# Graph attention with a mixture of experts on one core: flags between partitions prepared ahead, one scan for both directions, and the experts' layer norm on ScalarE

## The chip, the cores and the metric

The kernel runs on one core of one Trainium2 chip. The metric is the device time of one launch in microseconds; the time before is the median of three runs. Readings of the trace come from one more execution, which the hardware profiler recorded.

## What the reference computes

There are 30000 nodes with 256 features, 510000 edges sorted by their destination, 8 edge types and 4 heads. The layer is a graph attention followed by a small mixture of experts, each with a layer norm in front and a residual around it:

```python
feat = einsum('ni,rhid->rnhd', layernorm(x), conv_weights)      # one feature table per edge type
el = sum(feat[type, src] * attn_l[type]);  er = sum(feat[type, dst] * attn_r[type])
e  = leaky_relu(el + er, 0.2)
alpha = softmax of e over the edges that share a destination     # segment_max, exp, segment_sum
x  = x + segment_sum(alpha * feat[type, src]) + h_bias
y  = layernorm(x)
x  = x + shared_mlp(y) + (best 2 of 4 experts by softmax(y @ gW + gb), weighted)(y)
```

All results are f32.

## The kernel before, in words

**Features.** For every 128 nodes the kernel normalises x, transposes it (L292) and multiplies it with the weights of all types and heads (L305); the tables go to memory as `feat`, with one more column per head that holds the node's share of the score. Beside this, generators are advanced by hand through `aside`: `edge_records` prepares the records of the edges, `places` then works out in 21 batches of up to 12 blocks what each block of edges needs later, and `expert_weights` loads the experts. `places` writes one row of `WR` words per partition and block into `rk_d`: the row numbers to gather (`WI`), destinations (`WD`), marks (`WA`), penalties (`WP`), flags (`W1`) and types (`WT`). `first_rows` gathers the first edge row of each partition and block ahead of time and stores it in `stage`, four blocks to a store.

**Blocks.** Then 252 blocks of 2048 edges follow, 16 edges (`U`) on each of 128 partitions, and one last block (`UL` = 18). Edges of one destination lie next to each other, so they may run over several of a partition's columns and over several partitions. The softmax needs the largest score of a destination: `scores` runs one scan forward and one backward along the columns (L1033, L1034), with penalties of -1e30 where a destination starts. The value at the end of each partition's row is then passed on between partitions: `turn_ends` transposes 128x4 values for each direction (L1040, L1041), `across` scans 4x128 values forward (L1047) and backward (L1048), `turn_back` transposes both back (L1055, L1056), and `softmax` combines them (L1062 to L1065). For the scan over partitions, `flags_across` transposes a flag for each partition, which says that one destination fills it (L962), and copies it to `through` (L964); `flags` lays out the penalties and flags for it by four copies on ScalarE (L951, L952, L954, L955).

After the exponential (`exps`, L1071, with the copy L1072 into `ft`) the gathered rows are weighed on VectorE (L1079), one-hot matrices are made on ScalarE (L1010, L1011), and TensorE sums the rows by destination (L1086). `finish` divides, `residual_sum` adds x (L1117) and takes the statistics for the second layer norm (`stats`, L722 and L723).

**Order.** The program's order is written out by hand. Each block t has six slots. In slot 0 come `load(t + 2)`, `gather(t + 1)` and `flags(t + 1)`, in the later slots the steps of block t, and with each slot goes a sixth of the sums of block t - 1. `load` puts five DMAs into SP's queue (`rk` L903, `dr` L921, `erp` L924, `xt` L926 and `stage` L931 by `gather`), and `gather` 15 indirect DMAs into POOL's (L933), into a ring of four blocks' rows.

**Experts.** Four blocks share one pass of the experts. `Experts.steps` lists its steps, and one of them is taken in each slot once a group's last x1 is there: the square root (`spread`, L727), the scaling in two steps (`scale`, L731 and L734), two transposes (`turn`, L742, copied by ScalarE at L744), the layers (`layer`: matmuls L798, eviction with relu on ScalarE L799), the gates (L764 to L786), `experts2` (L823, L825, L829), the weighing (L838), and four times `last` (L851 to L854), whose result L857 adds to x1 and `put` (L1097) sends to the output from SP's queue.

The code after the blocks runs only if a flag found in the data asks for it; it did not in these runs.

Of the kernel before, what the change touches and what calls it, by code (L numbers as in the profile page):

```python
# [21 lines left out]
P = 128  # L22
# [22 lines left out]

WI, WD, WA, WP, W1, WT, WR = 0, U, 2 * U, 3 * U, 4 * U + 1, 6 * U + 3, 6 * U + 3 + U * 4

# [6 lines left out]
def kernel(  # L54
# [46 lines left out]
    dk_d = dram.tile([NBLK * CAP + 16], I16, name="dk_d")  # L101
    stage = dram.tile([NBLK * P, H * HW], F32, name="stage")
    exc_d = dram.tile([P], F32, name="exc_d")
    KT = -(-(NBLK + 1) // P)
# [25 lines left out]
    def layernorm(pool, xg, n, name, m=P):  # L130
# [10 lines left out]
        for t in range(n):  # L141
# [31 lines left out]
                   allow_small_or_imprecise_dtypes=True)  # L173
    NPEN = 3
    pens = []
    for i in range(NPEN + 1):
        f = wf.tile([P, H, U if i < NPEN else UL], F32, name=f"penf{i}")
        b = wf.tile([P, H, U if i < NPEN else UL], F32, name=f"penb{i}")
        nc.gpsimd.memset(f, -BIG)
        nc.gpsimd.memset(b, -BIG)  # L180
        pens.append((f, b))
    carry = []
    for i in range(2):
        cf = wf.tile([H, P + 1], F32, name=f"carf{i}")
        cb = wf.tile([H, P + 1], F32, name=f"carb{i}")
        nc.gpsimd.memset(cf, -BIG)
        nc.gpsimd.memset(cb, -BIG)
        carry.append((cf, cb))
    nc.gpsimd.memset(b3, 0.0)
# [32 lines left out]
    with ExitStack() as cx:  # L222
# [268 lines left out]
        def places(cl):  # L491
# [30 lines left out]
            fetch(0)  # L522
            yield
            done = None
            for k, (b0, n) in enumerate(batches):
# [32 lines left out]
                count["ready"] = b0 + n  # L558
                pen = kp.tile([P, GB, UW], F32, name="penk")[:, :n]
                nc.vector.tensor_scalar_mul(pen, rc[:, :, :, 3], -BIG)  # L560
                yield
                nc.gpsimd.tensor_copy(of[:, :, WP:WP + UW], pen)
                d16 = kp.tile([P, GB, U], I16, name="d16k")[:, :n]
                nc.gpsimd.tensor_copy(d16, rc[:, :, :U, 1])
                a1 = kp.tile([P, GB, UW], F32, name="a1k")[:, :n]
                a2 = kp.tile([P, GB, UW], F32, name="a2k")[:, :n]
                flat = "p b u -> p (b u)"
# [5 lines left out]
                nc.gpsimd.tensor_copy(of[:, :, W1:W1 + UW], a1)  # L573
                nc.gpsimd.tensor_copy(of[:, :, W1 + UW:W1 + 2 * UW], a2)
                yield
                th = o[:, :, WT:].bitcast(BF16).rearrange("p b (u r) -> p b u r", r=R)
# [5 lines left out]

                def done(o=o, d16=d16, b0=b0, n=n):
                    nc.sync.dma_start(rk_d[b0:b0 + n].rearrange("b p w -> p b w"), o)
                    nc.sync.dma_start(dk_d[b0 * CAP:(b0 + n) * CAP].rearrange("(b p u) -> p b u", p=P, u=U), d16)
# [18 lines left out]
        def first_rows():  # L604

            n, kept = 4, []
            fp = cl.enter_context(tc.tile_pool(name="first", bufs=3))
# [94 lines left out]
    class Experts:  # L702
# [3 lines left out]
        def __init__(self, pool, ph, pc, x1, n, put):  # L706
            self.pool, self.ph, self.pc, self.x1, self.n, self.put = pool, ph, pc, x1, n, put
            self.w = n * M
            self.mv = pool.tile([P, T, 2], F32, name="c_mv", bufs=2)

# [9 lines left out]
        def stats(self, t):  # L720
            st = self.pool.tile([P, 6], F32, name="c_st")
            nc.vector.bn_stats(st[:M], self.x1[:M, t, :])  # L722
            nc.vector.bn_aggr(self.mv[:M, t, :], st[:M])  # L723

        def spread(self):
            self.rs = self.pool.tile([P, T], F32, name="c_rs")
            nc.scalar.activation(self.rs[:M, :self.n], self.mv[:M, :self.n, 1], AF.Sqrt, bias=eps[:M])  # L727

        def scale(self, j):
            if j == 0:  # L730
                nc.vector.reciprocal(self.rs[:M, :self.n], self.rs[:M, :self.n])  # L731
                self.xn = self.pool.tile([P, T, D], F32, name="c_xn")
            for t in range(j, min(j + 2, self.n)):
                nc.vector.tensor_scalar(self.xn[:M, t, :], self.x1[:M, t, :], self.mv[:M, t, 0:1],  # L734
                                        self.rs[:M, t:t + 1], op0=ALU.subtract, op1=ALU.mult)

# [125 lines left out]
    with ExitStack() as cx:  # L862
# [16 lines left out]
        NCH = 6  # L879
        flat = "p h u -> p (h u)"  # L880
        blk = {}

        class Block:


            def __init__(self, t):
                self.u = U if t < NBLK else UL
                self.sc = [-(-self.u * c // NCH) for c in range(NCH + 1)]
                self.dw = -(-self.u * P // 48) * 16
                self.dc = [-(-self.u * c // 4) for c in range(5)]  # L890
                at = t % RING * U
                self.ft = ring[:, at:at + self.u]
                self.own = t < NBLK
                self.pens = pens[t % NPEN if t < NBLK else NPEN]

        def load(t):
# [3 lines left out]
            if s.own:  # L900
# [6 lines left out]
                s.mark, s.marki = rf[:, WA:WA + U], rk[:, WA:WA + U]  # L907
                s.pen = rf[:, WP:WP + U + 1]

# [27 lines left out]
        def flags(t):  # L937


            s = blk[t]  # L940
            n = s.u
            s.penf, s.penb = s.pens
            if not s.own:
                s.pen = wk.tile([P, UL + 1], F32, name="pen", bufs=1)[:, :n + 1]
                nc.vector.tensor_scalar_mul(s.pen, s.rc[:, :, 3], -BIG)
                s.a12 = wk.tile([P, 2, UL], F32, name="a12", bufs=1)
                nc.vector.tensor_tensor_scan(s.a12[:, 0], s.pen[:, :n], s.pen[:, :n], 0.0, ALU.min, ALU.min)
                nc.vector.tensor_tensor_scan(s.a12[:, 1, ::-1], s.pen[:, n:0:-1], s.pen[:, n:0:-1], 0.0,
                                             ALU.min, ALU.min)
            mid = s.pen[:, None, 1:n].to_broadcast([P, H, n - 1])  # L950
            nc.scalar.copy(s.penf[:, :, 1:], mid)  # L951
            nc.scalar.copy(s.penb[:, :, :n - 1], mid)  # L952
            ends = wk.tile([P, 2, H], F32, name="ends")
            nc.scalar.copy(ends[:, 0, :], s.a12[:, 0, n - 1:n].to_broadcast([P, H]))  # L954
            nc.scalar.copy(ends[:, 1, :], s.a12[:, 1, 0:1].to_broadcast([P, H]))  # L955
            s.ends = ends

        def flags_across(t):
            s = blk[t]
            pn = ps_p.tile([H, 2, P], F32, name="pn", tag="sm")  # L960
            for i in range(2):
                nc.tensor.transpose(pn[:, i, :], s.ends[:, i, :], ident)  # L962
            s.through = wk.tile([H, 2, P], F32, name="through")
            nc.scalar.copy(s.through, pn)  # L964
# [59 lines left out]
        def scores(t):  # L1024
# [4 lines left out]
            exchange(s, s.e)  # L1029
            s.fb = wk.tile([P, 2, H * UL], F32, name="fb")[:, :, :H * s.u].rearrange("p i (h u) -> p i h u", h=H)  # L1030
            s.f, s.b = s.fb[:, 0], s.fb[:, 1]
            e, f, b = s.e.rearrange(flat), s.f.rearrange(flat), s.b.rearrange(flat)
            nc.vector.tensor_tensor_scan(f, s.penf.rearrange(flat), e, -BIG, ALU.add, ALU.max)  # L1033
            nc.vector.tensor_tensor_scan(b[:, ::-1], s.penb.rearrange(flat)[:, ::-1], e[:, ::-1], -BIG,  # L1034
                                         ALU.add, ALU.max)

        def turn_ends(t):
            s = blk[t]
            s.t1 = ps_p.tile([H, 2, P], F32, name="t1", tag="sm")
            nc.tensor.transpose(s.t1[:, 0, :], s.f[:, :, s.u - 1], ident)  # L1040
            nc.tensor.transpose(s.t1[:, 1, :], s.b[:, :, 0], ident)  # L1041

        def across(t):

            s = blk[t]
            cf, cb = carry[t % 2]
            nc.vector.tensor_tensor_scan(cf[:, 1:], s.through[:, 0, :], s.t1[:, 0, :], -BIG, ALU.add, ALU.max)  # L1047
            nc.vector.tensor_tensor_scan(cb[:, P - 1::-1], s.through[:, 1, ::-1], s.t1[:, 1, ::-1], -BIG,  # L1048
                                         ALU.add, ALU.max)

        def turn_back(t):
            s = blk[t]
            cf, cb = carry[t % 2]
            s.t2 = ps_p.tile([P, 2, H], F32, name="t2", tag="sm")
            nc.tensor.transpose(s.t2[:, 0, :], cf[:, :P], ident[:H, :H])  # L1055
            nc.tensor.transpose(s.t2[:, 1, :], cb[:, 1:], ident[:H, :H])  # L1056

        def softmax(t):
# [3 lines left out]
            nc.vector.tensor_add(c, s.t2[:, :, :, None].to_broadcast(at), s.a12[:, :, None, :s.u].to_broadcast(at))  # L1062
            nc.vector.tensor_max(c, c, s.fb)
            nc.vector.tensor_max(s.f, c[:, 0], c[:, 1])
            nc.vector.tensor_sub(s.e, s.e, s.f)  # L1065
            exchange(s, s.e)
# [338 lines left out]
```

## Time and profile before

| | us |
|---|---|
| median of three runs (8380.45 to 8390.53) | 8389.48 |
| the profiled execution | 8380.65 |
| its span, first to last instruction | 8379.0 |
| busy: PE / DVE / ACT / POOL | 6330.2 / 5381.4 / 3416.7 / 4073.5 |
| mean granted TensorE clock | 0.877 |

PE is TensorE's matmuls, PEld its weight loads (which overlap), DVE VectorE, ACT ScalarE, POOL GpSimd and SP the queue that issues most DMAs. The span is the profiled execution without what lies around it. An idle time in the profile stands with the event that ended it ("releaser"); "remote" and "issue" are waits for which the profile shows no instruction of the program. The features reach to about 1750 us, and the blocks fill the rest; in the page's slices of 1/40 of the span this is slices 1 to 8 and 9 to 40.

### The profile page before, as it was taken

How to read it: one execution, taken by the hardware profiler on the slowest of the kernel's cores; microseconds unless marked ns; L12 is line 12 of the kernel's file. 1: busy time of each engine (PE TensorE's matmuls, PEld its weight loads, DVE VectorE, ACT ScalarE, POOL GpSimd, SP SyncE). 2: the span in 40 equal slices, each digit the busy share in tenths (PEclk: the TensorE clock that was granted, in tenths of full speed). 3: DMA queues.
4: the chain of work that ended last, by engine and by line, in shares of the span. 5: the costliest groups of instructions: out<-in, count | busy, mean ns of one | idle time of the engine just before them, and what ended most of it. 6: DMA issues, size and time to landing. Idle time of an engine off the chain costs nothing. (4 is left out here: it accounts for less than half of the span.)

```text
span 8379.0 us, 96556 instructions
## 1 busy us (share of the span) xinstructions
PE 6330.2 (76%) x25254; PEld 3986.0 (48%) x25255; DVE 5381.4 (64%) x13882; ACT 3416.7 (41%) x9511; POOL 4073.5 (49%) x4327
## 2 busy tenths in 40 slices
PE   9999999956666767777666667777666777777667
PEld 5555555534444444444444444444444444444444
DVE  5557774447666666666666666666666666666665
ACT  2222222224444444444444444444444444444444
POOL 1101114665555555555555555555555555555552
PEclk9999999978888888888888888888888888888888
DMA  6657778964444444444444444444444444444441
GB/s 226 229 177 238 224 243 303 341 197 123 116 117 117 118 116 119 119 121 119 117 120 117 119 116 118 118 123 118 118 116 117 118 119 118 116 119 117 115 118 55
DMA packets 761457, 1209.52 MB, mean 144 GB/s; under 512 B 241638, under 2 KB 599789, under 8 KB 730685
## 3 DMA queue, kind: packets, MB, share of 16 engines
q1 hardware_dynamic: 565453, 663.56, 24.8%
q0 software_dynamic: 194400, 539.40, 23.3%
q8 instruction: 206, 3.38, 0.2%
q14 instruction: 358, 2.93, 0.1%
q10 hardware_dynamic: 1040, 0.26, 0.0%
HBM read 818.57 MB, written 384.23 MB: 144 GB/s over the span
## 5 line engine op out<-in xcount | busy, mean ns | idle before, releaser
L933 POOL DMA_INDIRECT ft<-feat,rk x3798 | 3608.6, 950 | 2919.9 <-PE po L1086 956.0
L1086 PE MATMUL po<-ft,oh 128*128 128x260 f32 x8100 | 2305.4, 421 | 286.3 <-DVE ho L1107 149.5
L1086 PEld LDWEIGHTS po<-ft,oh 128*128 128x128 f32 x8100 | 1565.4, 208 | 569.7 <-issue 292.4
L305 PE MATMUL ps<-w,xT 128*128 128x448 f32 (+1 forms) x4700 | 1712.6, 519 | 14.3 <-DVE xT L294 8.6
L1079 DVE TENSOR_TENSOR ft<-ft,p 128x768 f32<-128x768 f32 x1518 | 1289.9, 850 | 394.8 <-issue 184.1
L1010 ACT ACTIVATE oh<-icol,rk 128x128 f32<-128x128 f32 x4032 | 1329.1, 389 | 66.4 <-remote 45.5
L305 PEld LDWEIGHTS ps<-w,xT 128*128 128x128 f32 x4700 | 877.3, 191 | 704.9 <-issue 613.5
L798 PE MATMUL ph<-xT,w 128*128 128x512 f32 (+1 forms) x512 | 372.1, 859 | 961.8 <-issue 888.7
L307 ACT COPY fo<-ps 128x448 f32<-128x448 f32 (+1 forms) x711 | 377.3, 533 | 1087.4 <-PE ps L305 912.4
L998 DVE TENSOR_TENSOR ere<-pe,rk 128x384 f32<-128x384 f32 x1008 | 553.3, 549 | 373.4 <-remote 247.9
L1011 ACT ACTIVATE oh<-oh 128x384 f32<-128x384 f32 x1518 | 740.2, 488 | 49.4
L987 PEld LDWEIGHTS <-ohT 128*128 128x128 bf16 x4050 | 393.9, 158 | 548.8 <-issue 438.1
L798 PEld LDWEIGHTS ph<-xT,w 128*128 128x128 f32 x512 | 112.3, 260 | 1112.1 <-issue 952.5
L744 ACT COPY xT<-ph 128x512 f32<-128x512 f32 (+1 forms) x128 | 73.1, 572 | 1325.3 <-remote 1299.9
L1000 DVE TENSOR_REDUCE e<-ere 128x16 f32<-128x384 f32 (+1 forms) x1012 | 561.5, 555 | 34.8
L987 PE MATMUL pe<-erp,ohT 128*128 128x96 bf16 x4050 | 442.3, 236 | 113.3 <-DVE ohT L970 73.5
L798 PE MATMUL ph<-xT,v 128*128 128x512 f32 (+1 forms) x1024 | 500.2, 613 | 2.3 <-ACT h L799 1.5
L1062 DVE TENSOR_TENSOR c<-t,rk 128x128 f32<-128x128 f32 x252 | 71.8, 285 | 618.9 <-remote 582.0
L1071 ACT ACTIVATE p<-e 128x64 f32<-128x64 f32 (+1 forms) x253 | 70.4, 278 | 844.9 <-DVE e L1022 741.8
L307 DVE COPY fo<-ps 128x448 f32<-128x448 f32 (+1 forms) x464 | 242.3, 528 | 221.9 <-PE ps L305 194.2
L1040 PE MATMUL t<-ident,fb 128*4 128x128 f32 x253 | 70.8, 280 | 383.6 <-DVE fb L1033 196.7
L851 PE MATMUL pf<-w,h 128*128 128x256 f32 x506 | 203.2, 491 | 189.1 <-ACT wT L844 85.1
(206 smaller groups left out, 7422.2 us busy)
## 6 DMA issues: line engine op xcount, KB each, us to landing
feat<-fo SPq DMA_DIRECT2D x234, 1040.0 KB
dr<-dk_d SPq DMA_DIRECT2D x252, 516.0 KB
ft<-feat,rk POOLq DMA_INDIRECT x3798
stage<-fr SPq DMA_DIRECT2D x63, 520.0 KB
ft<-stage SPq DMA_DIRECT2D x252, 130.0 KB
xt<-xb_d SPq DMA_DIRECT2D x253, 128.0 KB
out_dram<-og SPq DMA_DIRECT2D x253, 128.0 KB
xb_d<-xb SPq DMA_DIRECT2D x58, 512.0 KB
```

Of the source, the lines that this page charges most:

```text
L305: nc.tensor.matmul(ps, t["xT"][:, k, :], w[:, k, c0:c1], start=k == 0, stop=k == 1)
L307: eng(t["fo"][:, h0:h1, :HD], ps[:, :n].rearrange("p (a d) -> p a d", d=HD))
L798: nc.tensor.matmul(ps[:, :self.w], lhs, rhs, start=i == 0, stop=i == len(pairs) - 1)
L851: nc.tensor.matmul(pf[:M], self.h2[:, tok], w3, start=True, stop=False)
L933: nc.gpsimd.indirect_dma_start(out=s.ft[:, u].rearrange("p h d -> p (h d)"), out_offset=None, in_=feat[:, :], in_offset=bass.IndirectOffse ...
L987: nc.tensor.matmul(pe[:, u - u0].rearrange("p f r -> p (f r)"), s.ov[:, u, :], s.erp.rearrange("n h k r -> n (h k r)"), start=True, stop=True)
L998: nc.vector.tensor_mul(ere, s.pe[:, :u1 - u0], s.th[:, u0:u1, None, :].to_broadcast([P, u1 - u0, H * 3, R]))
L1000: nc.vector.tensor_reduce(s.e[:, :, u0:u1].rearrange("p h u -> p u h"), ere.rearrange("p u (h k) r -> p u h (k r)", h=H), AX.X, ALU.add)
L1010: nc.scalar.activation(s.oh[:, u, :], icol, AF.Abs, bias=s.nd[:, u:u + 1])
L1011: nc.scalar.activation(s.oh[:, u0:u1], s.oh[:, u0:u1], AF.Relu, bias=1.0, scale=-1.0)
L1079: nc.vector.tensor_mul(fc, fc, pc[:, :, None].to_broadcast([P, (u1 - u0) * H, HD]))
L1086: nc.tensor.matmul(s.po.rearrange("n h d -> n (h d)"), s.oh[:, u, :], s.ft[:, u].rearrange("p h d -> p (h d)"), start=u == 0, stop=u == s. ...
```

## The change

1. In `places`, the flags between partitions are worked out for all blocks of a batch at once: two matmuls (one against the identity, one against `turned`, an identity with its columns reversed) and one copy make rows of 2 x 128 values per block, which are stored in `thr_d`. `load` fetches them as `through`, 8 rows of 128, by one more DMA per block. `rk` now holds the penalties in both directions, so that one copy in `flags` lays them out. `flags_across` is left only for the last block.
2. Both scans across partitions become one of 8x128: the backward rows are turned by multiplying with `turned` in `turn_ends`, and a copy turns the result back.
3. The second layer norm goes to ScalarE: `stats` takes the sum by `Identity` with an accumulator, its mean with the sign turned, and the sum of squares by `Square`; `scale` uses `Identity` with a scale and a bias per row.
4. Around these, `places` starts after six turns instead of one, `penk`, `a1k` and `a2k` have one buffer, `first_rows` stores three blocks at a time, and `fb` and two sets of `pens` are kept for the whole run.

```diff
+    turned = wf.tile([P, P], F32, name="turned")
...
             fetch(0)
-            yield
+            for _ in range(6):
+                yield
...
-                nc.gpsimd.tensor_copy(of[:, :, WP:WP + UW], pen)
+                nc.gpsimd.memset(of[:, :, WP], -BIG)
+                nc.gpsimd.memset(of[:, :, WP + 2 * U - 1], -BIG)
+                for i in range(2):
+                    nc.gpsimd.tensor_copy(of[:, :, WP + 1 + i * (U - 1):WP + U + i * (U - 1)], pen[:, :, 1:U])
...
+                ps = pf.tile([P, 512], F32, name="ps")[:n, :2 * P]
+                nc.tensor.transpose(ps[:, :P], a1[:, :, U - 1], ident)
+                nc.tensor.matmul(ps[:, P:], a2[:, :, 1], turned, start=True, stop=True)
+                thr = kp.tile([GB, 2 * P], F32, name="thr")[:n]
+                nc.scalar.copy(thr, ps)
...
+                    nc.sync.dma_start(thr_d[b0:b0 + n].rearrange("b i p -> b (i p)"), thr)
...
-            n, kept = 4, []
+            n, kept = 3, []
...
         def stats(self, t):
-            st = self.pool.tile([P, 6], F32, name="c_st")
-            nc.vector.bn_stats(st[:M], self.x1[:M, t, :])
-            nc.vector.bn_aggr(self.mv[:M, t, :], st[:M])
+            st = self.st[:M, :, t:t + 1]
+            sq = self.pool.tile([P, D], F32, name="c_sq")
+            nc.scalar.activation(sq[:M], self.x1[:M, t, :], AF.Identity, accum_out=st[:, 0])
+            nc.scalar.activation(st[:, 1], st[:, 0], AF.Identity, scale=-1.0 / D)
+            nc.scalar.activation(sq[:M], self.x1[:M, t, :], AF.Square, bias=st[:, 1], accum_out=st[:, 2])
...
         def scale(self, j):
...
+                nc.vector.tensor_mul(rs[:, 1, :n], rs[:, 0, :n], self.st[:M, 1, :n])
...
-                nc.vector.tensor_scalar(self.xn[:M, t, :], self.x1[:M, t, :], self.mv[:M, t, 0:1],
-                                        self.rs[:M, t:t + 1], op0=ALU.subtract, op1=ALU.mult)
+                nc.scalar.activation(self.xn[:M, t, :], self.x1[:M, t, :], AF.Identity, bias=rs[:, 1, t:t + 1],
+                                     scale=rs[:, 0, t:t + 1])
...
         def load(t):
...
+                s.through = lp.tile([2 * H, P], F32, name="through", bufs=3)
+                h = thr_d[t]
+                nc.sync.dma_start(s.through, bass.AP(tensor=h.tensor, offset=h.offset, ap=[[P, 2], [0, H], [1, P]]))
...
         def flags(t):
...
+            if s.own:
+                nc.scalar.copy(s.pens, s.pen[:, :, None, :].to_broadcast([P, 2, H, n]))
+                return
...
+        def turned_rows(name, f, b):
+            t = ps_p.tile([2 * H, P], F32, name=name, tag="sm")
+            nc.tensor.matmul(t, f, ident, start=True, stop=False)
+            nc.tensor.matmul(t, b, turned, start=False, stop=True)
+            return t
...
         def turn_ends(t):
             s = blk[t]
-            s.t1 = ps_p.tile([H, 2, P], F32, name="t1", tag="sm")
-            nc.tensor.transpose(s.t1[:, 0, :], s.f[:, :, s.u - 1], ident)
-            nc.tensor.transpose(s.t1[:, 1, :], s.b[:, :, 0], ident)
+            rows = s.fb.rearrange("p i h u -> p (i h) u")
+            s.t1 = turned_rows("t1", rows[:, :2 * H, s.u - 1], rows[:, 2 * H:4 * H, 0])
...
         def across(t):
...
-            nc.vector.tensor_tensor_scan(cf[:, 1:], s.through[:, 0, :], s.t1[:, 0, :], -BIG, ALU.add, ALU.max)
-            nc.vector.tensor_tensor_scan(cb[:, P - 1::-1], s.through[:, 1, ::-1], s.t1[:, 1, ::-1], -BIG,
-                                         ALU.add, ALU.max)
+            nc.vector.tensor_tensor_scan(cf[:, 1:], s.through, s.t1, -BIG, ALU.add, ALU.max)
+            nc.vector.tensor_copy(cb, cf[:, P - 1::-1])
```

## The prediction

> **What bounds the kernel now.** I read the busy table and its slices first, then the windows of each stage, the windows of one group of four blocks, the waits of that group and last its timeline. The page says that the features (slices 1 to 8) and the blocks (slices 9 to 40) have different limits, and windows cut from each show it; columns are start:end, length, then busy us (and instructions) of PE, PEld, DVE, ACT and POOL, PE's granted clock, DMA share and GB/s:
>
> ```profile
> 400.00:1600.00 1200.00, 1191.40 (x3581) 646.90 (x3580) 723.53 (x1992) 306.92 (x654) 315.51 (x373) 1.00 0.77 249
> 4000.00:6000.00 2000.00, 1409.57 (x6199) 932.76 (x6198) 1346.42 (x3417) 917.07 (x2642) 1113.53 (x1172) 0.86 0.42 119
> ```
>
> The features are TensorE's: 1191 of 1200 us. In the blocks nobody is above 0.70, so the order of waits decides there. One group of four blocks, cut from one instruction of `exps` (L1071) to the next, gives this:
>
> ```profile
> 5001.86:5038.33 36.47, 14.40 (x65) 9.15 (x64) 17.34 (x42) 12.76 (x35) 24.64 (x26) 0.79 0.53 153
> 5038.33:5059.54 21.21, 19.34 (x85) 12.89 (x84) 18.24 (x53) 12.31 (x36) 13.58 (x15) 0.96 0.43 113
> 5059.54:5082.32 22.78, 18.10 (x85) 11.28 (x83) 16.84 (x39) 12.54 (x35) 15.07 (x16) 0.90 0.43 124
> 5082.32:5104.29 21.97, 21.18 (x86) 15.08 (x87) 17.01 (x41) 9.10 (x30) 3.81 (x5) 0.80 0.23 66
> ```
>
> Call them S (it scales and turns the group's x1), A, B and C (it writes the four outputs). S costs 14 us more than the others though TensorE, VectorE and ScalarE do no more in it. A and B leave TensorE 1.9 and 4.7 us idle and VectorE 3.0 and 5.9; C leaves TensorE 0.8. The timeline shows what S waits for (start, length, engine, line, what; idle time and its releaser in brackets):
>
> ```profile
> 5023.34 0.94 POOL L933 DMA_INDIRECT ft<-feat,rk  x1 [0.30 <-issue]
> ...
> 5025.84 0.95 POOL L933 DMA_INDIRECT ft<-feat,rk  x1 [0.30 <-issue]
> ...
> 5028.35 0.95 POOL L933 DMA_INDIRECT ft<-feat,rk  x1 [1.56 <-remote]
> 5031.15 0.95 POOL L933 DMA_INDIRECT ft<-feat,rk  x1 [1.86 <-issue]
> ...
> 5033.08 0.58 ACT L744 COPY xT<-ph 128x512 f32<-128x512 f32 x1 [21.43 <-remote]
> 5033.25 0.29 DVE L1062 TENSOR_TENSOR c<-t,rk 128x128 f32<-128x128 f32 x1 [7.79 <-remote]
> 5033.71 3.13 PE L798 MATMUL ph<-xT,w 128*128 128x512 f32 x3 [15.47 <-issue]
> ```
>
> ScalarE waits 21.4 us for a PE result, TensorE then 15.5 us for ScalarE, VectorE 7.8, and all three start within 0.7 us of each other, 2 us after POOL paused in a long row of gathers (0.95 us each, one per 1.25 us). That PE's results reach the others only when POOL pauses is my inference from this order; no row names it. POOL's long row exists because in C it stood idle 17.2 us: SP puts the outputs from 5087.98 to 5101, and the next `rk` (L903, 5101.94) queues behind them. So S ends by what POOL does, C by TensorE (21.2 of 22.0), A and B by a mix. Last, the rows that the change touches (busy us, mean ns, idle before):
>
> ```profile
> L722 DVE BATCH_NORM_STATS2 c_st<-x 128x6 f32<-128x256 f32 x253 | 108.3, 428 | 11.0 <-PE ph L798 2.5
> L723 DVE BATCH_NORM_AGGREGATE c_mv<-c_st 128x2 f32<-128x6 f32 x253 | 46.1, 182 | 8.7
> L734 DVE TENSOR_SCALAR c_xn<-x,c_mv,c_rs 128x256 f32<-128x256 f32 x253 | 93.9, 413 | 2.3
> L1048 DVE TENSOR_TENSOR_SCAN carb<-through,t 4x128 f32<-4x128 f32 x253 | 96.6, 382 | 0.0
> L962 PE MATMUL pn<-ident,ends 128*4 128x128 f32 x506 | 118.9, 324 | 0.0
> L964 ACT COPY through<-pn 4x256 f32<-4x256 f32 x253 | 88.8, 351 | 330.6 <-PE pn L962 233.5 <-remote 82.9 <-PE po L1086 11.8
> L727 ACT ACT_TABLE_LOAD x64 | 82.1, 1283 | 1.2
> ```
>
> **The parts, per group of four blocks (63 groups).**
>
> *Layer norm off VectorE.* It loses 4 x (0.43 + 0.18) = 2.4 us of statistics and 4 x 0.41 = 1.6 us of scaling, and gains a product of 128x4 per group (0.15 us, like the reciprocal L731). In S the stall swallows it: VectorE is idle 6.6 and 7.8 us there. In A, B and C the statistics stand in front of waits for PE (L764 1.2 us in A, L998 1.2 and L838 3.1 in B, L857 3.6 in C), which grow by what is saved. I realise 0 of 4.0. If VectorE is what PE's next step waits for, 0.61 per block comes back.
>
> *Layer norm onto ScalarE.* Three activations per block: two of 128x256 at about 0.44 us each (between 0.389 for 128x128, L1010, and 0.488 for 128x384, L1011) and a tiny one at 0.19 (L954): 1.07. One scaling per block: 0.44. Four flag copies become one of 128x128 (0.84 to 0.39), and L964's 0.35 goes. Net +0.71 per block: 46.7 busy of 102.4 us becomes 49.5, no bound by load. But order counts: the three wait for VectorE's sum x1 and stand before the next one-hots and the next eviction. The one-hots serve a block later; an eviction does not. The square-root table load (1.28 us, once a group), now hidden in the wait for x1, comes after `Square` and is bare; S hides it under the 21.4 us. Cost 0; the third rival is where this is wrong.
>
> A rule speaks against this part. The Trainium skill ("ScalarE: Activation LUTs", Rules for kernel authors) says that adds and multiplies belong on VectorE, which it calls faster per element, its figure being for bf16; the rows here put 128x256 f32 at 0.413 us on VectorE against about 0.44 on ScalarE, so no such gap shows. Its section on the table load has 186 ns + 0.833 ns per element + 93 ns for each pointer operand, by which (an estimate) the scaling would take 0.585 us instead of 0.44, some 37 us more of ScalarE's busy time over 253 blocks and none of the sum, where this time lies beside other work.
>
> *Flags worked out in the features.* PE loses two transposes a block: 0.22 to 0.65 us (0.11 us apart when queued, 0.324 each if not); I take 0.4. C is TensorE's, so it realises 0.4. In A and B both engines are nearly full, so the gain there lies between this 0.4 and the 0.18 that VectorE saves in the next paragraph: 0.3 each.
>
> *Two scans in one.* VectorE loses 0.38 (L1048) and gains a copy of 8x128: no such row exists; between 0.15 (128x4, L731) and 0.38 (the scan itself), and I take 0.2 as for 128x64 operations (0.22). Net -0.18. The matmuls at both ends keep their number.
>
> *The new load `through`.* One DMA per block of 8 rows between `rk` and `dr` in SP's queue, three buffers, so it waits for VectorE's `across` three blocks earlier. Behind it stand `dr`, `erp`, `xt` and `stage`, and then the next `rk`, which POOL needs. Today SP stops at `erp` instead (5032.99 to 5051.15 in A) and these serve a block later; I cost it at 0. If POOL's start slips by one gather, 1.25 us per group.
>
> *Features.* 42 more matmuls of 128 columns on a full TensorE at 90.0 / 470 = 0.19 us (transposes L292): +8 us, 5 to 12 by 0.11 and 0.28. 21 copies, 42 memsets and the split copy on POOL run beside it (ScalarE 307 and POOL 316 of 1200 us busy); 84 stores of three blocks replace 63 of four, same bytes.
>
> *Sum.* C -0.4, A and B -0.3 each, S 0: -1.0 x 63 = -63, +8 = -55 us. The profiled execution took 8380.65 us (span 8379.0), so 8325.7 of its kind; the median of the runs is 8.8 us above it, and from that median 8389.5 - 55 = **8334**. A measurement here tells about 0.2% (17 us) from no change.
>
> **Rivals.**
>
> *First (the forecast): most of the saving is absorbed.* Ends: all of 0.65 in A, B, C and 5 in the features, -118 us (8271); only 0.22 in C and +12, -2 us (8387). Chance 0.40, of it 0.06 within 0.2%.
>
> *Second: VectorE sets A, B and C.* It is at 0.67 in the blocks, and A and C have 18.2 and 17.0 of 21 to 22 us. Then 0.61 + 0.18 comes back three times: 2.37 x 63 = 149, +8: 8248. If S gives its part too, 4 x (0.61 + 0.41 + 0.18) - 0.15 = 4.65 x 63 = 293: 8104. Against it: the waits for PE named above. Chance 0.19.
>
> *Third, on the other side: ScalarE's waits stand before its evictions.* Each block's three activations wait for x1, and the eviction (L799, L825) queued behind them frees PE's next product. Price 1.07 us per block where that eviction is what PE waits for. It decides once the delay exceeds ScalarE's slack, today 3.1 us (h L799 waiting for PE). With one block the loss just eats the gain (8394 + 8, 8402); with two, 2.1 - 1.0 = 1.1 x 63 = 69, + 8: 8467; with three 2.2 x 63 + 8: 8537, and with the bare table load added 1.28 x 63 = 81 more. For it: A and B are tight, and the in-order engine gets a wait per block that it did not have. Against: ScalarE is 0.46 busy. Chance 0.33, 0.01 of it within 0.2%.
>
> *Fourth: nothing is realised.* A, B and C take 22.5, 22.0 and 22.5 us from one `exps` to the next, averaged over all groups, whatever they hold, and 15 gathers x 1.25 + two pauses of 1.7 make 22.2: POOL's rhythm may set all. Then only the features' +8: 8397. Chance 0.08.
>
> The page named above budgets 2.7 us for each switch of tables, against the 1.28 us of the row here; by it the third rival's last term would be 170 us, an estimate.
>
> **Numbers.** Faster 0.34 + 0.19 = 0.53; same 0.06 + 0.01 + 0.08 = 0.15; slower 0.32. The range leaves out the deeper part of the second (0.07) and the two dearer forms of the third (0.13): 8200 to 8480. The first case's own range is 8271 to 8387.
>
> **What would show it.** Right: S still near 36 us, its waits at L744 and L1062 as long; VectorE's busy share from 0.67 to about 0.62; C shorter by 0.4. Second: A, B and C each shorter by 0.8. Third: waits of PE at L798 for ScalarE grow in A or B, and ScalarE waits for x1. Wrong altogether: S shorter or longer by over 2 us, for then the row of gathers has moved.

## The result and the profile after

The changed kernel takes 8494.65 us (median of four runs, 8487.32 to 8510.81) against 8390.01 for the kernel before beside it: ratio 1.0129, 95% interval [1.0112, 1.0147]. The prediction said 8334, in a range of 8200 to 8480, with a chance of 0.32 for slower. It was wrong in its sign.

The runs fell on several chips. On some the kernel before takes 8370 to 8450 us, as in the prediction; on others the same kernel takes 6650 to 6660 ("quick chips" below). The two kinds are kept apart, by the time of the kernel before that ran on the same chip, and the result to be explained is that of the first kind.

The windows of the stages, as for the kernel before (start:end, length, busy us of PE, PEld, DVE, ACT, POOL, clock, DMA share, GB/s):

```profile
400.00:1600.00 1200.00, 1200.00 (x3636) 647.44 (x3635) 732.97 (x1991) 312.16 (x672) 311.57 (x419) 1.00 0.77 247
4000.00:6000.00 2000.00, 1439.45 (x6203) 946.11 (x6201) 1243.13 (x3120) 980.29 (x2728) 1078.88 (x1140) 0.85 0.40 116
```

VectorE fell from 0.67 to 0.62, as foreseen. But TensorE, which was to lose two transposes a block, rose from 1409.6 to 1439.5 of 2000 us, while 3% fewer gathers were issued (1140 against 1172). One group of four blocks, S, A, B and C, in the same columns:

```profile
4955.29:4992.03 36.74, 15.45 (x68) 9.70 (x67) 15.24 (x37) 15.50 (x39) 24.60 (x26) 0.79 0.49 140
4992.03:5013.60 21.57, 19.63 (x87) 13.14 (x86) 17.49 (x51) 12.90 (x37) 12.73 (x14) 0.96 0.42 120
5013.60:5036.40 22.80, 18.63 (x88) 11.25 (x86) 16.11 (x37) 13.09 (x37) 14.60 (x16) 0.93 0.47 132
5036.40:5060.55 24.15, 19.55 (x86) 13.77 (x87) 16.43 (x39) 9.76 (x31) 4.86 (x6) 0.93 0.22 62
```

Each group differs, so averages tell more. Over the 60 groups from the fifth block to the 245th (one start of `exps` to the next) S takes 36.2 us before and 35.9 after, A 22.5 and 24.2, B 22.0 and 22.2, C 22.5 and 22.5. In these two traces A carries the loss. A whole group takes 103.29 us before and 104.89 after: 60 x 1.60 = 96 of the 111 us between the two spans. Of the rest, 12 us arise before the fifth block (the second `exps` begins at 1844.9 before and at 1862.6 after) and 4 after the 245th.

Where TensorE's work comes from is in its groups. First the kernel before (busy us, mean ns, idle before):

```profile
L1040 PE MATMUL t<-ident,fb 128*4 128x128 f32 x253 | 70.8, 280 | 383.6 <-DVE fb L1033 196.7 <-issue 118.5 <-DVE e L1022 31.7
L1041 PE MATMUL t<-ident,fb 128*4 128x128 f32 x253 | 71.7, 283 | 0.0
L1055 PE MATMUL t<-ident,carf 4*128 4x4 f32 x253 | 55.5, 219 | 12.7 <-remote 8.0 <-DVE carb L1048 4.5
L1056 PE MATMUL t<-ident,carb 4*128 4x4 f32 x253 | 50.0, 198 | 0.0
```

and the same four calls in the changed kernel:

```profile
L990 PE MATMUL t<-ident,fb 128*8 128x128 f32 x506 | 101.7, 284 | 279.8 <-DVE fb L1069 153.9 <-DVE e L1058 101.2 <-DVE e L1056 15.2
L991 PE MATMUL t<-turned,fb 128*8 128x128 f32 x506 | 102.3, 286 | 0.0
L1088 PE MATMUL t<-ident,car 8*128 8x4 f32 x506 | 100.7, 267 | 39.6 <-issue 23.2 <-DVE car L1081 16.2
L1089 PE MATMUL t<-ident,turn 8*128 8x4 f32 x506 | 95.5, 257 | 0.0
```

Read the counts: 506 instead of 253. In these rows a transpose of f32 is one instruction per call and a plain f32 matmul is two, and the change made all four calls plain. The kernel before showed this already: `sums` (L1086) and `dest_expand` (L987) each call one matmul per edge column, 252 x 16 + 18 = 4050 calls, and the f32 one has twice the instructions of the bf16 one:

```profile
L1086 PE MATMUL po<-ft,oh 128*128 128x260 f32 x8100 | 2305.4, 421 | 286.3 <-DVE ho L1107 149.5
L987 PE MATMUL pe<-erp,ohT 128*128 128x96 bf16 x4050 | 442.3, 236 | 113.3 <-DVE ohT L970 73.5
```

What the four calls hold of TensorE is read from the timeline, from the first of them to the next other instruction; before:

```profile
5048.78 0.27 PE L1040 MATMUL t<-ident,fb 128*4 128x128 f32 x1 [1.87 <-DVE fb L1033]
5048.89 0.27 PE L1041 MATMUL t<-ident,fb 128*4 128x128 f32 x1
5049.00 0.59 PE L798 MATMUL ph<-xT,v 128*128 128x512 f32 x1
```

and after:

```profile
4790.88 0.39 PE L990 MATMUL t<-ident,fb 128*8 128x128 f32 x2 [2.03 <-DVE fb L1069]
4791.11 0.38 PE L991 MATMUL t<-turned,fb 128*8 128x128 f32 x2
4791.42 1.16 PE L814 MATMUL ph<-xT,v 128*128 128x512 f32 x2
```

0.22 us became 0.54. `turn_back` went in the same way from 0.21 (5055.03 to 5055.24) to 0.54 (4799.16 to 4799.70). These are typical: the medians over all blocks are 0.22, 0.54, 0.21 and 0.53. The two transposes of the flags that were taken away had held 0.22 in this block (5043.20 to 5043.42), 0.31 in the median. So a block has 0.65 us more of TensorE and 0.22 to 0.31 less, net 0.34 to 0.43, over 253 blocks 86 to 109 us.

VectorE's part of the single scan did get shorter, 0.402 + 0.229 us where the two scans took 0.401 + 0.382:

```profile
L1081 DVE TENSOR_TENSOR_SCAN car<-through,t 8x128 f32<-8x128 f32 x252 | 101.4, 402 | 139.6 <-PE po L1119 47.9 <-remote 38.8 <-issue 26.6
L1082 DVE COPY turn<-car 8x128 f32<-8x128 f32 x253 | 58.0, 229 | 8.7
```

### The profile page after: what moved, and what is told of

It is laid out like the page before. It is cut to its first block, busy times and chain, and to the rows that moved or that the text cites. A ratio compares the mean times of both kernels' runs of the same rounds, so it can differ in the third digit from the quotient of the medians.

```text
span 8490.1 us, 97792 instructions
## 1 busy us (share of the span) xinstructions
PE 6527.8 (77%) x25827; PEld 4095.4 (48%) x25828; DVE 5152.9 (61%) x13193; ACT 3713.5 (44%) x10042; POOL 4065.5 (48%) x4382
## 5 line engine op out<-in xcount | busy, mean ns | idle before, releaser
L1119 PE MATMUL po<-ft,oh 128*128 128x260 f32 x8100 | 2333.9, 425 | 274.3 <-DVE ho L1140 152.9
L304 PE MATMUL ps<-w,xT 128*128 128x448 f32 (+1 forms) x4700 | 1712.3, 519 | 1.8 <-DMA w<-_L_gnn_conv_weights_dram 1.8
L304 PEld LDWEIGHTS ps<-w,xT 128*128 128x128 f32 x4700 | 873.6, 190 | 687.6 <-issue 599.7
L814 PE MATMUL ph<-xT,w 128*128 128x512 f32 (+1 forms) x512 | 381.8, 879 | 832.2 <-issue 762.6
L814 PEld LDWEIGHTS ph<-xT,w 128*128 128x128 f32 x512 | 121.0, 267 | 998.2 <-issue 841.6
L814 PE MATMUL ph<-xT,v 128*128 128x512 f32 (+1 forms) x1024 | 528.4, 642 | 3.7 <-ACT h L815 2.9
L1023 PE MATMUL pe<-erp,ohT 128*128 128x96 bf16 x4050 | 442.9, 236 | 90.7 <-DVE ohT L1006 46.5
L867 PE MATMUL pf<-w,h 128*128 128x256 f32 x506 | 209.3, 503 | 328.3 <-ACT wT L860 245.7
L734 ACT ACTIVATE c_sq<-x 128x256 f32<-128x256 f32 x253 | 105.6, 417 | 794.6 <-DVE x L1150 441.2
L1095 DVE TENSOR_TENSOR c<-t,rk 128x128 f32<-128x128 f32 x252 | 72.3, 287 | 519.3 <-remote 473.7
```

Of the source, the lines that this page charges most:

```text
L304: nc.tensor.matmul(ps, t["xT"][:, k, :], w[:, k, c0:c1], start=k == 0, stop=k == 1)
L814: nc.tensor.matmul(ps[:, :self.w], lhs, rhs, start=i == 0, stop=i == len(pairs) - 1)
L867: nc.tensor.matmul(pf[:M], self.h2[:, tok], w3, start=True, stop=False)
L1023: nc.tensor.matmul(pe[:, u - u0].rearrange("p f r -> p (f r)"), s.ov[:, u, :], s.erp.rearrange("n h k r -> n (h k r)"), start=True, stop=True)
L1119: nc.tensor.matmul(s.po.rearrange("n h d -> n (h d)"), s.oh[:, u, :], s.ft[:, u].rearrange("p h d -> p (h d)"), start=u == 0, stop=u == s. ...
```

## The experiments

Theory 1 was the prediction's third rival: ScalarE's in-order wait for x1. Theory 2: the doubled f32 matmuls. Theory 3: SP's longer queue and the start of the blocks. The ratios to the kernel before on the same chip (several where a kernel ran more than once):

| kernel | before takes 6650 to 6660 us | before takes 8370 to 8450 us |
|---|---|---|
| layer norm on ScalarE only | 0.9891, 0.9893, 0.9917 | 0.9999 [0.9988, 1.0010] |
| loaded flags only | 1.0000, 1.0004 | not run there |
| flags and layer norm, two scans | 0.9913, 0.9929 | 1.0005 [0.9988, 1.0023] |
| flags and one scan, VectorE's layer norm | 1.0151, 1.0158 | 1.0134 [1.0117, 1.0151] |
| the whole change | 0.9963 [0.9950, 0.9975] | 1.0129 [1.0112, 1.0147] |
| the same, `turn_back` by transposes | not run there | 1.0099 [1.0074, 1.0123] |
| the same, `turn_ends` twice | not run there | 1.0298 [1.0280, 1.0316] |
| the same, statistics back on VectorE | 1.0150 [1.0133, 1.0167] | not run there |
| the same, statistics a slot later | 1.0046 [1.0029, 1.0062] | not run there |

**The layer norm back on VectorE.** The edit puts the old bodies of `stats`, `spread` and `scale` back:

```diff
-            nc.scalar.activation(sq[:M], self.x1[:M, t, :], AF.Identity, accum_out=st[:, 0])
...
+            nc.vector.bn_stats(st[:M], self.x1[:M, t, :])
+            nc.vector.bn_aggr(self.mv[:M, t, :], st[:M])
```

> The changed kernel with the whole layer norm of the experts back on VectorE (bn_stats, bn_aggr, scaling); flags, one scan and the features as changed. Theory 1 (ScalarE's in-order wait for x1 is the loss): the changed kernel's 24.2 us in block A falls back to about 22.5 and the time by 80 to 100 us, to about 8400 us. Theory 2 (the f32 matmuls of the turned rows, which the trace of the changed kernel shows as two instructions each, 506 rows where there were 253, load TensorE in A): at most 30 us come back, about 8470. Theory 3 (the start of the blocks and the longer queue of SP): under 20 us, about 8480.

6758.86 us, beside a kernel before of 6660.47. Theory 1 expected a fall, and the time is 1.5% above before. The same kernel, later, with what was expected:

> The changed kernel with the layer norm back on VectorE (loaded flags, one scan). Beside a kernel before of 8380 to 8450: theory 2 keeps the loss of the one scan, +1% or more; theory 1 (ScalarE's layer norm is a part of the loss): +0.5% or less. Beside 6657: 6755 again.

8488.13 beside 8372.86: the whole loss is there without any layer norm on ScalarE. Its block A takes 24.0 us on average, as in the changed kernel.

**Only the layer norm on ScalarE** (the reverse edit, in the kernel before).

> The kernel before with only the layer norm of the experts moved to ScalarE. Theory 1: the loss appears here nearly whole, 8390 + 80 to 100 = about 8480 us, with a wait of ScalarE for x1 in each block. Theories 2 and 3: within 30 us of 8390, since neither the matmuls nor the queue of SP change.

> The kernel before with only the layer norm on ScalarE. Beside a kernel before of 8380 to 8450, theory 2 with the savings absorbed (waits for PE results take what VectorE saves): within 0.5% of before; if ScalarE's wait for x1 costs there, +0.8% or more. Beside 6657: 6587 again.

6586.4 us beside 6660.47, and 8376.09 beside 8372.86. It gains 1.1% on quick chips and nothing on the others; it costs nowhere, which ends theory 1. Its gathers on a quick chip show what stops the gain there:

```profile
L939 POOL DMA_INDIRECT ft<-feat,rk x3193 | 3027.6, 948 | 972.8 <-issue 347.0 <-PE po L1092 259.0 <-PE pe L993 70.7
```

In the 4000 us from 2000 to 6000 POOL issued 3193 gathers, one per 1.253 us, and no wait of POOL that the trace lists was over 0.3 us: 60 gathers make 75.2 us, and a group takes 75.25. It is the fastest version measured on those chips, ahead of both kernels, and level with the kernel before on the others.

**Two scans again,** flags loaded and layer norm on ScalarE. The transposes come back in `turn_back` and, for the flags, in `places` too, and `through` is loaded as 4 rows of 2 x 128 (not all lines are shown):

```diff
-            s.t1 = turned_rows("t1", rows[:, :2 * H, s.u - 1], rows[:, 2 * H:4 * H, 0])
+            s.t1 = ps_p.tile([H, 2, P], F32, name="t1", tag="sm")
+            nc.tensor.transpose(s.t1[:, 0, :], s.fb[:, 0, :H, s.u - 1], ident)
+            nc.tensor.transpose(s.t1[:, 1, :], s.fb[:, 1, :H, 0], ident)
...
+            nc.vector.tensor_tensor_scan(cf[:, 1:], s.through[:, 0, :], s.t1[:, 0, :], -BIG, ALU.add, ALU.max)
```

> The changed kernel with two scans of 4x128 and transposes again in place of one scan of 8x128 and the turned matmuls; flags are still loaded, layer norm still on ScalarE. Theory 2: TensorE's busy time falls by 0.2 ms over the run (four more instructions a block at 0.2 to 0.28 us) and the time by 60 us or more, to about 8430. Theory 1: VectorE gains 0.15 us a block and TensorE loses some of what nobody waits for, so 8495 within 25 us.

> The changed kernel with two scans and transposes (all second passes gone). Theory 2: 8340 to 8410 beside a kernel before of 8380. Theory 1 (layer norm on ScalarE): 8490 within 30. Beside 6657: 6600 again.

6600.89 beside 6660.47, and 8447.93 beside 8448.37. With the single scan and its plain matmuls gone the loss is gone: 1.24% between the two ratios, or 104 of 8390 us (they come from different chips). The additional load, the later start and the layer norm on ScalarE are all still in this kernel, so theory 3 goes with theory 1. The edit takes out the scan and the matmuls together, but VectorE's rows of the single scan are the shorter ones, as shown above, and POOL's gathers take 0.95 us in all these kernels; what grew is TensorE's instructions. That fits theory 2. On quick chips the single scan costs 0.5% beside ScalarE's layer norm (0.9913 to 0.9963) and 1.5% beside VectorE's (1.0000 to 1.0151).

**The suspected cost doubled.**

```diff
-            s.t1 = turned_rows("t1", rows[:, :2 * H, s.u - 1], rows[:, 2 * H:4 * H, 0])
+            for _ in range(2):
+                s.t1 = turned_rows("t1", rows[:, :2 * H, s.u - 1], rows[:, 2 * H:4 * H, 0])
```

> The changed kernel with the turned matmuls of turn_ends made twice, which doubles the suspected cost: four more TensorE instructions of 0.19 us a block, the result being the same. Theory 2 (TensorE's time sets the blocks of the changed kernel): 0.5 us or more a block, 253 x 0.5 = 125 us more than the changed kernel, about +1.5% against before where that stands at -0.37%. If the chain of waits rather than TensorE's time is what costs: 0.2 us or less a block, under 50 us, +0.4% or less.

8620.03 beside 8376.89, 1.69% above the changed kernel's ratio, some 140 us. That is close to 253 x 0.54 = 137 us of TensorE, but partly by luck, for the edit adds more than matmuls. The tile `t1` comes from a pool with one buffer (`ps_p`, bufs=1), and the second set often starts long after the first:

```profile
4808.04 0.39 PE L990 MATMUL t<-ident,fb 128*8 128x128 f32 x2 [2.07 <-DVE e L1058]
4808.27 0.38 PE L991 MATMUL t<-turned,fb 128*8 128x128 f32 x2
4811.89 0.60 PE L990 MATMUL t<-ident,fb 128*8 128x128 f32 x2 [3.23 <-issue]
```

Over the run TensorE stands idle for 348 us before the second sets, 239 of them in S. So more turned matmuls cost time here, and how much of it is TensorE's time and how much these waits is not shown. The run doesn't tell TensorE's load from a later result either, since the second set delays both.

**Half of it taken away:** `turn_back` transposes all 8 rows and uses 4 of each.

```diff
-            nc.tensor.matmul(s.t2[:, 0, :], cf[:, :P], ident[:2 * H, :H], start=True, stop=True)
+            nc.tensor.transpose(t2[:, 0, :], cf[:, :P], ident[:2 * H, :2 * H])
```

> The changed kernel with turn_back by transposes of the 8 rows (one TensorE instruction each in place of two f32 passes); turn_ends keeps its four. Theory 2: two TensorE instructions fewer a block, some 0.25 us, 40 to 60 us less than the changed kernel: 6580 to 6610 beside a kernel before of 6657, 8430 to 8460 beside one of 8380. If the layer norm or the loaded flags cost instead: the changed kernel's 6634 or 8495 within 15.

8541.57 beside 8448.37. The gain of 0.3% (25 us) against the changed kernel's ratio is smaller than the 40 to 60 us expected and than the 253 x 0.32 = 81 us of TensorE taken off (0.54 against 0.22 in its trace), and the two intervals overlap: the direction fits, the size is not shown. More firmly, this run and the one with two scans ran on the same chip: 1.0099 against 1.0005, 0.94% or 79 us of 8448, with transposes in `turn_back` in both. So most of the loss lies in `turn_ends` and the scan behind it, where TensorE's added 0.54 - 0.22 = 0.32 us a block make 81 us.

**The whole change and the flags alone, on a quick chip.**

> The changed kernel itself, unaltered, beside the kernel before. The four runs so far came with a kernel before of 6660 us instead of 8390, in which TensorE is 0.88 busy in the blocks and POOL's gathers follow each other without pauses (15 x 1.253 = 18.8 us a block, in the runs with the layer norm on ScalarE). Theory 2 (the doubled turned matmuls on a busy TensorE cost, the layer norm on ScalarE gains): if the kernel before takes 6660 again, the change lies between the run without the layer norm (+98) and the run without the one scan (-60): 6660 + 20 to 60. Theory 1 (the layer norm on ScalarE is the loss): above the run without it, 6760 or more. If the kernel before takes 8390, 8495.

> The kernel before with only the flags worked out in the features and loaded (with the stores of three blocks and the later start of that work); two scans and VectorE's layer norm as before. Theory 2: TensorE loses two transposes a block and nothing is added, so 20 to 60 us less than before in the blocks and some 15 more at their start: 6660 gives 6620 to 6660 (8390 gives 8350 to 8400). Theory 3 (the added load in front of SP's queue delays what POOL needs): 30 us or more above before.

6634.5 and 6657.96 beside 6657.27. Here the change as a whole gains 0.37%, because the layer norm gives more than the one scan takes. Theory 2 had put it at 20 to 60 us above the kernel before, as the middle between two other runs, and so missed the sign; the two parts don't add up there. The flags give nothing measurable, where theory 2 expected 20 to 60 us less in the blocks.

**Which part of the layer norm, and does ScalarE's wait cost?** Two runs on quick chips.

> The changed kernel with only the statistics (bn_stats, bn_aggr) back on VectorE; the scaling stays on ScalarE. Theory 1: the wait for x1 goes from ScalarE in all four blocks, so nearly all that the whole layer norm gives back comes back here: 8400 to 8420 us. If instead the scaling on ScalarE (0.585 us each in the trace of the changed kernel) is what costs, 8480.

> The changed kernel with ScalarE's three statistics moved from slot 0 to slot 1 of each block, behind slot 0's one-hots and eviction (the experts' steps begin one slot later). Where the kernel before takes 6660 us and the changed one -0.37%: theory 1 (the wait for x1 in ScalarE's order costs) expects another 30 us or more less, -0.8% or better; theory 2 (the doubled turned matmuls cost, the wait is hidden) expects within 15 us of the changed kernel. Where the kernel before takes 8390 and the changed one +1.29%: theory 1 expects it near +0.5%, theory 2 near +1.3%.

With only the statistics back on VectorE all of the gain is lost (6758.53, as with the whole layer norm back): in the changed kernel there the scaling on ScalarE is worth nothing and the statistics all of it. With the statistics one slot later ScalarE's wait for x1 falls, from 269.0 to 91.4 us in 2000 us of the trace (the waits' total, times and longest; first the changed kernel, then the one with late statistics, both on quick chips):

```profile
ACT c_sq L734 <- DVE x L1150: 269.0, 105, 2.9
```

```profile
ACT c_sq L734 <- DVE x L1151: 91.4, 78, 1.9
```

and the time grows by 0.8% against the changed kernel's ratio, where theory 1 expected a gain and theory 2 no change within 15 us: both missed. The edit also moves all steps of the experts by a slot (block C grows from 19.2 to 21.4 us), so it doesn't price the wait by itself.

**Repeats.** Four of these kernels ran once more. The expectations have the slower kind in mind, but the chip was a quick one; the layer norm alone had been repeated before:

> The changed kernel with two scans and transposes again (flags loaded, layer norm on ScalarE), now meant for where the kernel before takes 8380 us. Theory 2 (the doubled f32 matmuls of the turned rows; doubling them once more cost 1.7% there): 1 to 1.5% below the changed kernel, so 8340 to 8410. Theory 1 (layer norm on ScalarE): 8490 within 30. Beside 6660: 6600 as before.

> The kernel before with only the layer norm on ScalarE, where the kernel before takes 8380 us. Theory 1: +0.8% or more, 8450. Theory 2: no loss, 8300 to 8390. Beside 6660: 6587.

> The changed kernel with the layer norm back on VectorE (flags loaded, one scan), where the kernel before takes 8380 us. Theory 1: 8390. Theory 2: the loss stays or grows, 8480 or more. Beside 6660: 6759.

> The kernel before with only the loaded flags, where the kernel before takes 8380 us. Theory 2: two transposes fewer a block, 8300 to 8390. Theory 3 (the added load in SP's queue or the later start): 8400 to 8450. Beside 6660: 6658.

> The kernel before with only the layer norm on ScalarE, again, to see whether its -1.09% holds beside another kernel before. Theory 2: where the kernel before takes 6660 us, 6586 again, since POOL's 15 gathers of 1.253 us set 18.8 us a block; where it takes 8390, faster than before too, by 0.2 to 1%. Theory 1: where it takes 8390, slower by 0.8% or more.

They gave 6601.8, 6595.03, 6752.05 and 6653.61 beside 6653.19, and 6588.86 beside 6658.36: the first readings hold.

**The kernel before, profiled again.**

> The kernel before, unaltered, profiled where it takes some 6660 us. Every theory: no 20 us waits in the turn block, POOL nearly without pauses, TensorE near 0.88 busy in the blocks, and a group of four blocks at (6660 - 1760) / 63.25 = 77.5 us. Theory 2 adds: TensorE, not POOL, is what the group waits for, with POOL pausing 2 to 3 us a group above 4 x 18.8 = 75.2.

This was a chip of the first kind, 8375.59 us, with a group at 103.25 us: the trace that the prediction read is typical of that kind. Of the kernel before on a quick chip there is no trace, so what bounds it there stays open.

## Why the prediction was wrong

*The step that failed* is one sentence of the part on the two scans: "The matmuls at both ends keep their number." The calls keep their number, the instructions do not: 4 became 8 a block, 0.65 us of TensorE where the sum had 0. The loss of the single scan, 1.24% of 8390 = 104 us, is about two thirds of 253 x 0.65 = 164. That it comes with the single scan is shown by the runs; that TensorE's instructions are the reason within it follows from the rows, where no other instruction of the single scan grew, and from the run with `turn_ends` twice, which is not a clean price.

*The gains of the sum,* 0.4 in C and 0.3 in A and B for the two transposes and the shorter scan, did not come. The two transposes of the flags held 0.31 us of TensorE in the median, inside the 0.22 to 0.65 that was given, but with flags and layer norm and two scans the ratio is 1.0005: the time added to TensorE was paid for the most part, the time taken off it gave nothing. The flags are made a block ahead of their use; whether that is why is not shown.

*Right:* nothing of the layer norm's 4.0 us a group is realised on this kind of chip (0.9999), S stays at 36 us, and the new load `through` cost nothing that shows. The waits for TensorE's results in S are there still, though not "as long": VectorE's 618.9 us before L1062 became 519.3, and ScalarE's 1315.0 before L744 became 1067.0:

```profile
L760 ACT COPY xT<-ph 128x512 f32<-128x512 f32 x126 | 72.7, 577 | 1067.0 <-remote 1055.1 <-PE po L1119 4.5 <-issue 3.9
L1095 DVE TENSOR_TENSOR c<-t,rk 128x128 f32<-128x128 f32 x252 | 72.3, 287 | 519.3 <-remote 473.7 <-PE po L1119 29.2 <-PE ph L814 8.1
```

*The third rival* named a time near the result (8467 for two blocks) by a mechanism that isn't it: the layer norm on ScalarE alone costs nothing. ScalarE does wait for x1 (441.2 us before L734, below), but the sign that the rival named, TensorE waiting longer for the evictions, did not come: its idle time before the products with `v` (L798, now L814), almost all of it ended by these evictions, was 2.3 us in the whole run before and is 3.7 after.

*ScalarE's terms were too small.* The rows of the changed kernel:

```profile
L734 ACT ACTIVATE c_sq<-x 128x256 f32<-128x256 f32 x253 | 105.6, 417 | 794.6 <-DVE x L1150 441.2 <-DVE ere L1034 185.0 <-issue 93.7
L734 ACT ACTIVATION_READ_ACCUMULATOR c_sq<-x 128x1 f32 x253 | 47.1, 186 | 0.0
L735 ACT ACTIVATE c_st<-c_st 128x1 f32<-128x1 f32 x253 | 51.3, 203 | 8.0
L736 ACT ACTIVATE c_sq<-x,c_st 128x256 f32<-128x256 f32 x253 | 128.6, 508 | 8.2
L736 ACT ACTIVATION_READ_ACCUMULATOR c_sq<-x,c_st 128x1 f32 x253 | 47.3, 187 | 0.0
L750 ACT ACTIVATE c_xn<-x,c_rs 128x256 f32<-128x256 f32 x253 | 136.2, 585 | 10.0 <-DVE c_rs L747 10.0
```

The statistics take 0.417 + 0.186 + 0.203 + 0.508 + 0.187 = 1.50 us a block where 1.07 was put; each accumulator is read by an instruction of its own. The scaling takes 0.585 where 0.44 was put; VectorE had taken 0.413. The 0.585 is the figure that the Trainium skill's price ("ScalarE: Activation LUTs", What ACT_TABLE_LOAD costs) gave, and the trace agrees with it. The prediction took a value between two rows with fewer pointer operands (a scale or bias that is read per partition): L1010 has one, L1011 none. And its 0.488 for L1011 is the mean of two shapes, 0.523 for 128x384 and 0.417 for 128x256, the very shape that was wanted. Neither error moved the time on this kind of chip, where the layer norm on ScalarE alone gives 0.9999.

*The features.* +8 us was put. Here too calls were counted: the 21 plain matmuls against `turned` (L581) are 42 instructions. Yet TensorE's last matmul of the features ends 5 us earlier instead (1740.98 against 1746.23), with 14.3 us of idle time before L305 and 1.8 before L304 after. What came instead is at the start of the blocks: SP's last store of `stage` is issued at 1757.55 instead of 1747.41, and the second `exps` starts 18 us later, the fifth 12.

*Open:* which wait passes the added TensorE time on, and why it shows in A and not in C. The split moves between runs: with `turn_back` by transposes S takes 34.6 us and A 26.0, with `turn_ends` twice S 34.2, A 26.1 and C 23.9, so a group's total says more than A alone. One wait of TensorE goes with the loss in most kernels: at the start of C it waits for the gates (`wT`), whose copy stands right behind `exps` in ScalarE's order. This took 85.1 us of the run before and 245.7 after, 212.8 and 221.1 in the other two kernels with one scan, and 90.7 and 121.1 with the layer norm alone and with two scans. But with `turn_ends` twice it is 84.1, so it is not the whole account. Open too is what makes the two kinds of chip; none was met at two different times, so it may be the chip or its condition then. On the quick kind the traces show neither the 20 us waits in S nor POOL's pauses, with gathers of the same 0.95 us, and a granted clock of 0.96 to 0.98 in the blocks where the other kind has 0.82 to 0.86; which of these is cause and which effect is not shown.

## What to carry to other kernels

Price a changed call by the instructions that it becomes, and look for a row of the same kind in the profile before: there the f32 transposes had one instruction per call and the plain f32 matmuls two. A transpose that is turned into a multiplication with a permutation is no longer a transpose. On the chain between engines here the added instructions were paid for the most part, where the two transposes taken off beside it gave nothing back. And where a saving is absorbed by one chip's waits, it may be real on another: the layer norm on ScalarE is worth 0 on one kind and 1.1% on the other, until POOL's gathers set the pace.

## What the runs showed of the hardware

One program differed by 26% between chips: 8376.89 us and 6657.27 for the kernel before. The features don't differ (in the changed kernel's traces TensorE is busy for 1200 of 1200 us on the one and 1000 of 1000 on the other, at a clock of 1.00 and with 3.03 instructions per us on both), the blocks do. A plain f32 matmul that moves 128 columns over 8 stationary ones held TensorE 0.27 us; an f32 transpose that moves 128 over 4 held 0.11. In this trace an activation on ScalarE with an accumulator was followed by an instruction of 0.186 us that reads it.
